# Six gather buffers in place of nine in a deformable-convolution and expert kernel

## The chip, the cores and the metric

The kernel runs on one core of a Trainium2 chip. The metric is the device time of one execution in microseconds (us). A core has a matrix engine (TensorE, PE in the profile), a vector engine (VectorE, DVE), an activation engine (ScalarE, ACT), GpSimd (POOL), and SyncE (SP), which issues most plain transfers. Each works through its own queue of instructions in order and waits on semaphores for the others. GpSimd here does hardly anything but issue gathers, that is, transfers whose source rows come from a list of indices.

## What is computed

The input `x` has 4 images of 256 channels and 64x64 pixels. It is normalised over channels, then goes through three deformable 3x3 convolutions (each samples 9 positions per pixel, displaced by offsets that a small ordinary convolution computes, and interpolates between four neighbours). The result is added to `x`. Each pixel then becomes a token of 256 values that goes through the two best of eight experts (256 to 512 to 256 with a GELU), and that is added too.

```
def _deform_layer(x, w_off, b_off, w, b, dilation=1):
    om = lax.conv_general_dilated(x, w_off, ...) + b_off[None, :, None, None]
    off = om[:, :2 * K].reshape(B, K, 2, H, W)
    mask = jax.nn.sigmoid(om[:, 2 * K:])
    ...
    sampled = _bilinear(x, ys, xs) * mask[:, None]
    out = jnp.einsum('bikhw,oik->bohw', sampled, wk) + b[None, :, None, None]
...
x = x + _L0_conv_ref(_ln_c(x), ...)
t = t + _L0_ffn_ref(_ln_t(t), ...)   # top 2 of 8 experts, weighted by softmax
```

## The kernel before

**Tiling.** A pixel block is 512 pixels (8 rows of an image, `BLK`), handled as 4 groups of 128 pixels on the 128 partitions. Per block, 9 taps times 4 groups make 36 samples; 3 layers x 4 images x 8 blocks x 36 = 3456 samples in all.

**One sample** (`samples`, from line 489). The features of a layer lie in a table in device memory, in which one row of 4 KB holds the four neighbours of a position, each of 256 float32 values. GpSimd gathers 128 such rows into a tile `g` of 4 KB per partition (line 503). VectorE interpolates between neighbours along one axis, in place (line 509), then along the other into a smaller tile `s` (line 514), which is the last reading of `g`. ScalarE scales `s` by the mask (line 517). TensorE transposes `s` (line 532), ScalarE copies the transposed pair of samples to `sT` (line 535), and TensorE multiplies it with the tap's weights and accumulates (line 549).

```
g = self.gat.tile([P, 2, 2, C], F32, tag="g", ...)
self.gathered = nc.gpsimd.indirect_dma_start(out=g..., in_=self.table(...), in_offset=...idx[:, j : j + 1]...)
nc.vector.scalar_tensor_tensor(g[:, :, 0, :], g[:, :, 1, :], cf[:, j, 0:1], g[:, :, 0, :], ...)
s = self.smp.tile([P, C], F32, tag="s", ...)
self.last = nc.vector.scalar_tensor_tensor(s, g[:, 1, 0, :], cf[:, j, 1:2], g[:, 0, 0, :], ...)
nc.scalar.activation(s, s, AF.Copy, scale=cf[:, j, 2:3])
```

**Buffers around it.** The pool `gat` gives out `GB` tiles `g` in turn (line 147); a gather into a tile has to wait until line 514 has read what was in it. `s` has 8 tiles, and TensorE takes pairs of samples `LAG` = 2 pairs after they are put into VectorE's queue. Tiles and the orders of the queues are worked out when the kernel is built, from the program's order and from which buffers are free.

**Who else uses the pool.** In the first phase the normalisation puts its input and output blocks into the same tiles (`room`, line 188). At the end, the last group of tokens gathers its experts' outputs into them (`combine_fetch`, line 911).

**Work in between.** The kernel weaves other work between the samples: the offset convolution of the next layer's blocks (`off_block`), storing a layer's result into the tables (`store_table`), token normalisation and routing (`tokens`, `route`, `invert`), the experts (`expert`), and the weighted sum of their outputs (`combine`). Three lanes hand out pieces of it per tap, at a pace per group of tokens. VectorE's pieces are put behind the newest `self.last`, GpSimd's behind the newest `self.gathered`. On GpSimd, one step of an expert fetches a weight tile `w` (line 803) and two token tiles `zt` (line 815), and the sums fetch `gy` (line 918), all in the same queue as the gathers. On VectorE, line 895 adds a bias to an expert's output `y`, and lines 395 to 427 work out positions, indices and coefficients of a later block.

Of the kernel before, what the change touches and what calls it, by code (L numbers as in the profile page):

```python
# [34 lines left out]
FT_LOG = 8  # L35
FT = 1 << FT_LOG
FU = FT // P
GB = 9
LAG = 2
LEAST = 2.0**-30  # L40
WINN = CC * (RPB + 2) * W
# [76 lines left out]
class Weave:  # L118
# [3 lines left out]
    def __init__(self, ctx, tc, ins, out):  # L122
# [7 lines left out]
        def pool(name, bufs, **kw):  # L130
            return ctx.enter_context(tc.tile_pool(name=name, bufs=bufs, **kw))
# [14 lines left out]
        self.smp = pool("smp", 8)  # L146
        self.gat = pool("gat", GB)
        self.ps = pool("ps", 3, space=bass.MemoryType.PSUM)
# [999 lines left out]
```

## Time and profile before

| | us |
|---|---|
| median of 3 runs | 6531.28 (6528.49 to 6531.62) |
| the profiled execution, its own time | 7434.65 |
| span of its page | 7432.9 |
| scaling `s`, line 517, ACT, 3456 times | 1630.8 busy |
| interpolation into `s`, line 514, DVE, 3456 times | 1656.7 busy |
| weights product, line 549, PE, 6912 times | 3442.6 busy |
| transposes of `s`, line 532, PE, 6912 times | 1227.0 busy |

The profile is of one execution, which took 14% longer than the runs without one. Rows of groups give the source line, the engine, what is written and read, how many instructions, their busy time and mean duration, and then the idle time of the engine before them with what ended it. "issue" there means that the profile shows nothing that was waited for. A busy TensorE isn't one at its peak[...].

### The profile page before, as it was taken

How to read it: one execution, taken by the hardware profiler on the slowest of the kernel's cores; microseconds unless marked ns; L12 is line 12 of the kernel's file. 1: busy time of each engine (PE TensorE's matmuls, PEld its weight loads, DVE VectorE, ACT ScalarE, POOL GpSimd, SP SyncE). 2: the span in 40 equal slices, each digit the busy share in tenths (PEclk: the TensorE clock that was granted, in tenths of full speed). 3: DMA queues.
4: the chain of work that ended last, by engine and by line, in shares of the span. 5: the costliest groups of instructions: out<-in, count | busy, mean ns of one | idle time of the engine just before them, and what ended most of it. 6: DMA issues, size and time to landing. Idle time of an engine off the chain costs nothing. (4 is left out here: it accounts for less than half of the span.)

```text
span 7432.9 us, 88104 instructions
## 1 busy us (share of the span) xinstructions
PE 6352.4 (85%) x26500; PEld 3653.7 (49%) x26500; DVE 4932.4 (66%) x11467; ACT 3278.3 (44%) x7139; POOL 4441.2 (60%) x4245
## 2 busy tenths in 40 slices
PE   7888888888888898988877898898887889977887
PEld 3434443444445555555444454454554456644665
DVE  7767776888756666776855676666787554667521
ACT  3444444554444444554443444444453334444322
POOL 4555665666656665555666665665667664666543
PEclk8999999989999999999989999999998899988988
DMA  8889999999879888888888998888998876887644
GB/s 286 312 297 339 346 339 346 362 345 340 321 267 322 311 315 315 310 314 296 282 295 306 327 331 299 318 324 314 325 342 307 281 273 233 286 301 271 229 138 124
DMA packets 805210, 2228.40 MB, mean 300 GB/s; under 512 B 105016, under 2 KB 307768, under 8 KB 798976
## 3 DMA queue, kind: packets, MB, share of 16 engines
q0 software_dynamic: 551200, 1947.35, 73.0%
q1 hardware_dynamic: 253536, 275.41, 11.0%
q8 instruction: 214, 3.51, 0.2%
q14 instruction: 260, 2.13, 0.1%
HBM read 2165.40 MB, written 196.40 MB: 318 GB/s over the span
## 5 line engine op out<-in xcount | busy, mean ns | idle before, releaser
L503 POOL DMA_INDIRECT g<-tab,idx x3456 | 3650.6, 1056 | 2310.7 <-DVE s L514 975.8
L549 PE MATMUL acc<-sT,wk 128*128 128x512 f32 x6912 | 3442.6, 620 | 44.6 <-ACT r L580 17.0
L509 DVE SCALAR_TENSOR_TENSOR g<-g,cf 128x512 f32<-128x512 f32 x3456 | 2556.5, 743 | 274.2 <-DMA g<-tab,idx 249.9
L514 DVE SCALAR_TENSOR_TENSOR s<-g,cf 128x256 f32<-128x256 f32 x3456 | 1656.7, 482 | 1287.5 <-PE tp L532 561.4
L535 ACT COPY sT<-tp 128x512 f32<-128x512 f32 x1728 | 1010.7, 586 | 2052.0 <-PE tp L532 1137.3
L532 PE MATMUL tp<-ident,s 128*128 128x128 f32 x6912 | 1227.0, 287 | 635.7 <-ACT s L517 373.8
L517 ACT ACTIVATE s<-s,cf 128x256 f32<-128x256 f32 x3456 | 1630.8, 508 | 260.7 <-DVE s L514 157.0
L549 PEld LDWEIGHTS acc<-sT,wk 128*128 128x128 f32 x6912 | 1238.3, 200 | 916.2 <-issue 871.5
L532 PEld LDWEIGHTS tp<-ident,s 128*128 128x128 f32 x6912 | 880.9, 147 | 1607.0 <-issue 839.5
L859 PE MATMUL ph<-fzT,w 128*128 128x256 f32 x2608 | 683.7, 401 | 111.1 <-ACT hT L869 74.2
L877 PE MATMUL py<-w,hT 128*128 128x256 f32 x2608 | 658.8, 392 | 39.9 <-ACT hT L869 23.2
L859 PEld LDWEIGHTS ph<-fzT,w 128*128 128x128 f32 x2608 | 498.1, 200 | 256.2 <-ACT hT L869 92.7
L869 ACT ACTIVATE hT<-ph,w 128x256 f32<-128x256 f32 x652 | 279.2, 471 | 695.2 <-PE ph L859 388.3
L877 PEld LDWEIGHTS py<-w,hT 128*128 128x128 f32 x2608 | 486.6, 194 | 180.6 <-issue 69.4
L815 POOL DMA_INDIRECT zt<-z,tok x326 | 330.9, 1015 | 174.2 <-issue 90.3
L803 POOL DMA_INDIRECT w<-in_W,wrow x163 | 175.7, 1078 | 379.3 <-ACT sT L535 134.1
L357 PE MATMUL po<-win,wo 128*32 128x504 f32 (+1 forms) x2304 | 364.1, 613 | 11.2 <-issue 8.3
L918 POOL DMA_INDIRECT gy<-ys,slots x256 | 260.2, 1017 | 106.7 <-issue 79.7
L895 DVE TENSOR_TENSOR y<-py,w 128x512 f32<-128x512 f32 x163 | 111.8, 686 | 316.3 <-PE py L877 242.7
L366 ACT ACTIVATE om<-po,bo 128x512 f32<-128x512 f32 x96 | 66.0, 688 | 365.4 <-PE po L357 228.5
L357 PE MATMUL po<-win_pre,wo 128*32 128x504 f32 (+1 forms) x1152 | 191.2, 628 | 4.1 <-ACT om L366 3.3
L357 PEld LDWEIGHTS po<-win,wo 128*32 128x32 f32 x2304 | 74.4, 111 | 223.8 <-issue 190.5
(154 smaller groups left out, 3029.2 us busy)
## 6 DMA issues: line engine op xcount, KB each, us to landing
tab<-hv SPq DMA_DIRECT2D x512, 128.0 KB
g<-tab,idx POOLq DMA_INDIRECT x3456
ys<-y SPq DMA_DIRECT2D x163, 256.0 KB
tab<-h_pre SPq DMA_DIRECT2D x128, 256.0 KB
wk<-in_conv_w SPq DMA_DIRECT2D x117, 256.0 KB
xc_pre<-in_x SPq DMA_DIRECT2D x32, 512.0 KB
xr_tok<-in_x SPq DMA_DIRECT2D x32, 512.0 KB
t<-t_tok SPq DMA_DIRECT2D x32, 512.0 KB
```

The source lines that it names most:

```text
L357: nc.tensor.matmul(po[g * Q : (g + 1) * Q, :].rearrange("q (r w) -> q r w", w=W)[:, :, x0:x1], lhsT=self.wo[l][:, 3 * ky + kx, c, :], rhs= ...
L503: self.gathered = nc.gpsimd.indirect_dma_start(out=g.rearrange("p x s f -> p (x s f)"), out_offset=None, in_=self.table(*self.stages[i][:2 ...
L509: nc.vector.scalar_tensor_tensor(g[:, :, 0, :], g[:, :, 1, :], cf[:, j, 0:1], g[:, :, 0, :], ALU.mult, ALU.add,)
L514: self.last = nc.vector.scalar_tensor_tensor(s, g[:, 1, 0, :], cf[:, j, 1:2], g[:, 0, 0, :], ALU.mult, ALU.add)
L517: nc.scalar.activation(s, s, AF.Copy, scale=cf[:, j, 2:3])
L532: self.turned = nc.tensor.transpose(tp[:, c, u * P : (u + 1) * P], ss[u][:, c * P : (c + 1) * P], self.ident)
L535: nc.scalar.copy(self.sT[:, :, t0 * P : (t0 + 2) * P], tp)
L549: nc.tensor.matmul(self.acc[:, o, :], lhsT=self.wk[k][:, c, o * P : (o + 1) * P], rhs=sT[:, c, :], start=(k == 0 and c == 0), stop=(k == K ...
L815: self.nc.gpsimd.indirect_dma_start(out=zt, out_offset=None, in_=grp.zd, in_offset=bass.IndirectOffsetOnAxis(ap=grp.tok[:, j : j + 1], axi ...
L859: nc.tensor.matmul(ph[:, h, :], lhsT=w1[:, o : o + P], rhs=zT[:, c, :], start=(c == 0), stop=(c == CC - 1),)
L869: nc.scalar.activation(ht[:, h, :], ph[:, h, :], AF.Gelu, bias=w1[:, k : k + 1])
L877: nc.tensor.matmul(py[:, u, :], lhsT=hT[h // 2][:, h % 2, u * P : (u + 1) * P], rhs=w2[:, h * C : (h + 1) * C], start=(h == 0), stop=(h == ...
```

## The change

One constant is changed. The pool has six tiles `g` of 4 KB per partition where it had nine, so a gather waits for line 514 of the sample six back, not nine back. The first phase and the last group of tokens, which borrow the tiles, have six too. No instruction's operation or shape changes, and the 12 KB per partition that this leaves over are not used.

```
 FU = FT // P
-GB = 9
+GB = 6
 LAG = 2
```

## The prediction

> **What bounds the kernel now.** I read the page first (engine shares, slices, groups), then the list of waits, then the gather tile `g` by itself, then two stretches of the timeline. The page's first part, in busy us, share of the span and number of instructions:
>
> ```profile
> span 7432.9 us, 88104 instructions
> PE 6352.4 (85%) x26500; PEld 3653.7 (49%) x26500; DVE 4932.4 (66%) x11467; ACT 3278.3 (44%) x7139; POOL 4441.2 (60%) x4245
> DMA  8889999999879888888888998888998876887644
> ```
>
> TensorE carries the span, but not alone: PE has some 1080 us idle, and the DMA engines are busy eight or nine tenths nearly everywhere. The gather is where the change acts. Two rows of the groups (busy and mean ns, then idle time ahead and what ended most of it):
>
> ```profile
> L503 POOL DMA_INDIRECT g<-tab,idx x3456 | 3650.6, 1056 | 2310.7 <-DVE s L514 975.8
> L509 DVE SCALAR_TENSOR_TENSOR g<-g,cf 128x512 f32<-128x512 f32 x3456 | 2556.5, 743 | 274.2 <-DMA g<-tab,idx 249.9
> ```
>
> GpSimd waits 975.8 us for a buffer (L514 is the last reader of `g`); VectorE waits only 249.9 us for a gather. So today the buffers are usually full and gathers are early. The list of waits (us in total, times, longest) says how often:
>
> ```profile
> ACT sT L535 <- PE tp L532: 1137.3, 843, 7.3
> POOL g L503 <- DVE s L514: 975.8, 457, 15.4
> POOL g L503 <- issue: 801.9, 2420, 2.5
> ...
> DVE s L514 <- PE tp L532: 561.4, 349, 9.7
> ...
> PE tp L532 <- ACT s L517: 373.8, 174, 15.9
> ...
> DVE g L509 <- DMA g<-tab,idx: 249.9, 98, 10.3
> ```
>
> VectorE runs dry 98 times in 3456. VectorE also waits for PE (561.4 us) more than PE waits for samples on this row (373.8 us): the two take turns holding each other. The tile's own answer, with first and last start:
>
> ```profile
> L503 POOL DMA_INDIRECT g<-tab,idx x3456: 940/974/5220, 90.2 to 6990.8; - x192
> L509 DVE SCALAR_TENSOR_TENSOR g<-g,cf x3456: 644/745/816, 94.4 to 6997.8; 128x512 f32<-128x512 f32 x192
> ```
>
> The first gather is used 4.2 us after GpSimd starts it (nothing else in the rings), the last 7.0 us after. The mean demand is (6997.8-94.4)/3456 = 2.00 us per gather. How fast gathers can follow each other, and what starvation looks like, from the timeline of GpSimd and of VectorE (start, duration, idle before):
>
> ```profile
> 6876.12 0.96 POOL L918 DMA_INDIRECT gy<-ys,slots  x1 [0.30 <-issue]
> 6877.38 0.95 POOL L503 DMA_INDIRECT g<-tab,idx  x1 [0.30 <-issue]
> 6878.63 0.95 POOL L503 DMA_INDIRECT g<-tab,idx  x1 [0.30 <-issue]
> ```
>
> ```profile
> 6882.40 0.75 DVE L509 SCALAR_TENSOR_TENSOR g<-g,cf 128x512 f32<-128x512 f32 x1 [6.83 <-DMA g<-tab,idx]
> 6883.29 0.48 DVE L514 SCALAR_TENSOR_TENSOR s<-g,cf 128x256 f32<-128x256 f32 x1
> ```
>
> GpSimd's burst rate is one gather per 1.25 us. The gather started at 6877.38 is used at 6882.40: 5.02 us, with VectorE standing 6.83 us for it.
>
> **What the Trainium skill says.** "DMA: Bandwidth & Descriptors", section "Anatomy of one DMA — SWDGE (gpsimd) path", fits a GpSimd DMA with 2.0 us plus bytes/436e3. A gather is 128 rows of 4 KB, 524288 bytes, so the estimate is 2.0+1.2 = 3.2 us. The first gather of the trace agrees: 4.2 us less 0.95 us on GpSimd is 3.25 us. The same page, "Issuing engines are not separate DMA queues", says that DMAs of all issuing engines interleave on the same 16 DMA engines; the growth from 4.2 to 5.0 and 7.0 us in traffic fits that, although no row separates the cause. "Perfetto Trace Analysis", section "Optimization Strategy", says that a gap that keeps recurring on the engine that ought to be saturated can mean too few buffers. In this trace the recurring buffer gap is on GpSimd, which isn't the saturated engine.
>
> **The change part by part.** No instruction is added or removed; 3 tiles of 4 KB per partition go.
>
> *Steady flow: nothing.* A buffer is held from the gather's start to the end of L514, and GpSimd takes it 0.27 us later (an L514 from 3007.70 to 3008.17 releases a gather at 3008.44). L509's start to L514's end is 1.37 us in the two lines above. The loop is thus 4.2+1.37+0.27 = 5.8 us empty, 6.7 us at the 5.02 us gather, 8.6 us at the last one's 7.0 us. Six buffers pass one gather per 0.97, 1.11 or 1.44 us; nine pass one per 0.65 to 0.96 us. All are under the mean demand of 2.00 us. What six lose is stock: GpSimd leads by up to 3 gathers less, 3x1.28 = 3.8 us in a burst and 6 us at mean demand.
>
> *Bursts.* VectorE does a sample in 1.28 us when it is free (L509 at 3018.11, 3019.39, 3020.67). At the 7.0 us end the six-buffer loop of 1.44 us is 0.16 us slower. GpSimd issued 2420 gathers back to back ("issue" above), so the most that this can cost is 2420x0.16 = 387 us; at 5.02 us per gather it costs nothing.
>
> *Cover for GpSimd's other work.* A fetch puts three other DMAs between gathers (3016.13 to 3021.29 instead of 1.28 us later: 3.9 us), 163 times over the kernel. Nine buffers hide that; with six, a loop of 6.7 us plus 3.9 us is 10.6 us for six samples, 1.77 us each: hidden at mean demand, 2.9 us short in a burst. Where the fetch itself waits for its weight buffer, nothing is lost: GpSimd comes to it with fewer gathers out, but it leaves at the same moment.
>
> *The sum.* The two overlap, so I count them together over the trace's rows. For each gather I move its start to 0.27 us after the end of the L514 six gathers back, where it was earlier than that, keep its landing time as the DMA packets show it, and compare with when L509 took it. 671 of 3456 L509s would then be late, in 242 runs whose largest latenesses sum to 270 us: 144 us before 1950 us (no fetch there yet), 126 us after. Of the first part most are threes in which L509 ran ahead of L514 by several samples while `s` had no room (L509 four times in a row at 1796.2 to 1798.5); there VectorE was about to stand anyway, so I keep a third, 48 us. VectorE is late by 174 us. How much reaches PE? There are eight `s` buffers and PE works two pairs behind, so short delays are absorbed when PE is behind. I take the ratio of the two opposite waits, 373.8/(373.8+561.4) = 0.40: 70 us. The profiled execution took 7434.65 us, so 7505 us; the three runs' median of 6531.28 us is 0.878 of it, and scaled the cost is 62 us: **6593 us**, 0.9% slower.
>
> *Later fetches.* The weight and token fetches stand in GpSimd's queue behind a gather that now starts later, by 4.8 us on average where it is moved. PE waits today 15.9+10.0 us for weights, so they mostly have room; their bound is 0 to 50 us, I take 0.
>
> *Start and tail.* The first phase borrows the same tiles for its input blocks; three blocks are loaded ahead and two more tiles are in use, which fits in six. In the tail, the last group's combine borrows up to eight in place of gathers; the seventh waits until the first is summed, some 24 fetches of 1.28 us later. Both at nothing; at most one 5 us landing each.
>
> **Rivals.**
> A. Absorbed: PE is 85% busy with a denser schedule unprofiled (6352 us of busy PE against a 6531 us run, if it were the same work), so VectorE's lateness is swallowed. Against it stand the 174 PE waits for samples. 6531 us, within 13 us.
> B. The loop becomes the bound in bursts, as at the 7.0 us gather: 387 us on VectorE, 0.7 of it through because PE then runs dry for long, 271 us profiled, 238 us scaled: 6770 us. For it: the DMA engines at nine tenths. Against: fewer gathers out also means shorter queues in the rings.
> C. Faster. The order of VectorE's queue is fixed when the kernel is built and depends on which buffers are then free. In 210 samples (counted in the rows) L509s stand ahead of an earlier sample's L514; with three buffers fewer, less of this 0.74 us work can stand ahead of the side work that PE and GpSimd wait for (the sum `y`, positions). If all of it moved back, 210x0.74 = 155 us of that work would come earlier; a quarter on PE's path is 39 us, 34 scaled: 6497 us. It decides if VectorE's wait for gathers grows by less than 39/0.40 = 98 us. Against it: the run-ahead happens where VectorE had nothing better to do.
>
> **How the numbers follow.** The forecast (slower by 0.2 to 2.5%) has 0.56, A 0.12, B 0.17, C 0.15. About 0.2% is what a measurement of this kernel can tell from no change. So faster 0.15, same 0.12, slower 0.73. The forecast's own range is 6545 to 6695 us; to leave no more than 2 in 10 out, it reaches to C's 6497 and halfway into B: 6495 to 6740 us.
>
> **What would show it.** VectorE's wait for gathers at L509 grows from 249.9 to 400 us or more and from 98 to 200 times or more; GpSimd's wait for L514 grows well over 975.8 us, to several thousand; PE's wait for `s` grows by some 70 us; busy times and counts stay. I am wrong if L509's wait stays under 350 us (A or C), or if L509's spacing in undisturbed bursts goes from 1.28 to 1.4 us (B), or if VectorE's order of L509 and L514 has changed so much that the rows can't be compared.

## The result and the profile after

With six buffers the kernel takes **6712.36 us** (median of 4 runs, 6705.84 to 6723.06) where it took 6531.03 us with nine: a ratio of 1.028 (95% interval 1.0264 to 1.0296), 181 us slower. The forecast was 6593 us. The sign was right and the time lies in the wider range, but the loss is three times the 62 us of the forecast.

One fact is needed to read the numbers below: the same kernel with nine buffers took about 6530 us in some groups of runs and 7404 to 7522 us in others, and the profile that the prediction was made from (7434.65 us) is of the long kind, so each experiment is compared only with the nine-buffer runs of its own group. What stands opposite the profile after (6723.06 us) is therefore a nine-buffer execution of 6529.06 us (`base_d`).

The page of the nine-buffer kernel in the short group, first its shares, then three of the groups:

```profile
span 6527.2 us, 88104 instructions
PE 6078.2 (93%) x26500; PEld 3548.0 (54%) x26500; DVE 4956.1 (76%) x11467; ACT 3327.0 (51%) x7139; POOL 4423.9 (68%) x4245
...
L503 POOL DMA_INDIRECT g<-tab,idx x3456 | 3623.7, 1049 | 1546.1 <-issue 602.0
...
L509 DVE SCALAR_TENSOR_TENSOR g<-g,cf 128x512 f32<-128x512 f32 x3456 | 2559.3, 743 | 465.5 <-DMA g<-tab,idx 459.7
...
L532 PE MATMUL tp<-ident,s 128*128 128x128 f32 x6912 | 1191.9, 280 | 194.9 <-ACT s L517 192.8
```

The same lines of the page after, with six:

```profile
span 6720.8 us, 88230 instructions
PE 6137.5 (91%) x26500; PEld 3551.9 (53%) x26500; DVE 5013.5 (75%) x11467; ACT 3363.6 (50%) x7139; POOL 4494.3 (67%) x4245
...
L503 POOL DMA_INDIRECT g<-tab,idx x3456 | 3688.7, 1067 | 1683.9 <-issue 536.4
...
L509 DVE SCALAR_TENSOR_TENSOR g<-g,cf 128x512 f32<-128x512 f32 x3456 | 2570.9, 745 | 865.4 <-DMA g<-tab,idx 852.0
...
L532 PE MATMUL tp<-ident,s 128*128 128x128 f32 x6912 | 1218.5, 281 | 305.2 <-ACT s L517 299.3
```

The counts of work are the same and the mean durations of the gather chain's work nearly so. What grows is idle time ahead of L509, by 400 us, and 392 us of that end on a gather. On TensorE, idle time (span less busy) goes from 6527.2-6078.2 = 449.0 to 6720.8-6137.5 = 583.3 us, 134 us more, of which the wait of L532 for `s` is 106.5 us. PE's busy time grows by 59 us for the same 26500 matmuls. The two, 193.6 us, are the difference of the spans.

The list of waits (us in total, times, longest), nine buffers:

```profile
...
ACT s L517 <- DVE s L514: 611.0, 663, 8.9
POOL g L503 <- issue: 602.0, 1926, 0.7
...
DVE g L509 <- DMA g<-tab,idx: 459.7, 407, 10.4
POOL g L503 <- DVE s L514: 361.2, 317, 12.8
```

and six:

```profile
...
ACT s L517 <- DVE s L514: 939.7, 1013, 8.8
DVE g L509 <- DMA g<-tab,idx: 852.0, 897, 10.3
...
POOL g L503 <- issue: 536.4, 1760, 0.3
POOL g L503 <- DVE s L514: 464.5, 406, 10.6
```

What grew is VectorE's wait for gathers: from 407 times to 897, +392 us. It passes to ScalarE (L517) almost undiminished, +329 us, and from there in part to TensorE. GpSimd's own wait for a buffer grows only from 361.2 to 464.5 us. The last column tells what sort of starvation it is: the longest wait has not grown, there are just many more short ones, 0.95 us each on average (852.0/897).

How fast samples are used, by the gather tile itself (first and last start), nine buffers and then six:

```profile
L509 DVE SCALAR_TENSOR_TENSOR g<-g,cf x3456: 642/744/821, 96.0 to 6109.5; 128x512 f32<-128x512 f32 x192
```

```profile
L509 DVE SCALAR_TENSOR_TENSOR g<-g,cf x3456: 645/746/821, 97.4 to 6303.2; 128x512 f32<-128x512 f32 x192
```

(6109.5-96.0)/3456 = 1.74 us per sample with nine, 1.80 us with six. In the profile of the prediction it was 2.00 us. The first sample comes 1.4 us later, and behind the last one the span goes on for 417.7 us with nine and 417.6 with six: the start and the tail cost next to nothing, as forecast. And by stage, for L509 alone (stretch, length, busy and number on VectorE, granted PE clock, share of the DMA engines, GB/s), nine buffers, then six:

```profile
100.00:1100.00 1000.00, 497.12 (x672) 0.99 1.01 391
1700.00:6300.00 4600.00, 1802.37 (x2429) 0.98 0.93 341
```

```profile
100.00:1100.00 1000.00, 477.13 (x642) 0.99 0.99 374
1700.00:6300.00 4600.00, 1844.70 (x2477) 0.98 0.93 341
```

In the first stretch, where no expert fetches its weights yet, nine buffers bring 672 samples in 1000 us, one per 1.49 us, with the DMA engines busy all the time (1.01). Six bring 642, one per 1.56 us. (The later stretch has more samples with six because more of them are then left to do.) Counted by sample over the rows, six are 94 us behind after 1080 of the 3456 samples, about when the first fetches come (1741.9 us with nine, 1709.8 us with six); 139 us after 2592; 194 us at the end. Half of the loss is thus made in a third of the samples, in a stage with hardly a fetch.

A stretch of that kind on VectorE with six buffers (start, duration, idle before):

```profile
1502.81 0.75 DVE L509 SCALAR_TENSOR_TENSOR g<-g,cf 128x512 f32<-128x512 f32 x1 [1.14 <-DMA g<-tab,idx]
1503.69 0.48 DVE L514 SCALAR_TENSOR_TENSOR s<-g,cf 128x256 f32<-128x256 f32 x1
1504.09 0.74 DVE L509 SCALAR_TENSOR_TENSOR g<-g,cf 128x512 f32<-128x512 f32 x1
1504.97 0.48 DVE L514 SCALAR_TENSOR_TENSOR s<-g,cf 128x256 f32<-128x256 f32 x1
1506.49 0.75 DVE L509 SCALAR_TENSOR_TENSOR g<-g,cf 128x512 f32<-128x512 f32 x1 [1.03 <-DMA g<-tab,idx]
```

and what TensorE does meanwhile:

```profile
1500.02 1.88 PE L549 MATMUL acc<-sT,wk 128*128 128x512 f32 x4
1501.73 0.97 PE L532 MATMUL tp<-ident,s 128*128 128x128 f32 x6
1504.77 0.64 PE L532 MATMUL tp<-ident,s 128*128 128x128 f32 x2 [2.06 <-ACT s L517]
```

In these lines VectorE waits about a microsecond for two gathers out of three, and PE stands 2.06 us for the sample that comes of it.

### The profile page after: what moved, and what is told of

Its sections match the earlier page's. It is cut to its first block, busy times and chain, and to the rows that moved or that the text cites. A ratio compares the mean times of both kernels' runs of the same rounds, so it can differ in the third digit from the quotient of the medians.

```text
span 6720.8 us, 88230 instructions
## 1 busy us (share of the span) xinstructions
PE 6137.5 (91%) x26500; PEld 3551.9 (53%) x26500; DVE 5013.5 (75%) x11467; ACT 3363.6 (50%) x7139; POOL 4494.3 (67%) x4245
## 5 line engine op out<-in xcount | busy, mean ns | idle before, releaser
L503 POOL DMA_INDIRECT g<-tab,idx x3456 | 3688.7, 1067 | 1683.9 <-issue 536.4
L549 PE MATMUL acc<-sT,wk 128*128 128x512 f32 x6912 | 3336.0, 603 | 13.7 <-ACT win L580 9.9
L509 DVE SCALAR_TENSOR_TENSOR g<-g,cf 128x512 f32<-128x512 f32 x3456 | 2570.9, 745 | 865.4 <-DMA g<-tab,idx 852.0
L517 ACT ACTIVATE s<-s,cf 128x256 f32<-128x256 f32 x3456 | 1691.2, 509 | 1019.8 <-DVE s L514 939.7
L514 DVE SCALAR_TENSOR_TENSOR s<-g,cf 128x256 f32<-128x256 f32 x3456 | 1657.7, 482 | 362.9 <-PE tp L532 49.5
L549 PEld LDWEIGHTS acc<-sT,wk 128*128 128x128 f32 x6912 | 1196.5, 194 | 839.9 <-issue 800.2
L535 ACT COPY sT<-tp 128x512 f32<-128x512 f32 x1728 | 1009.8, 585 | 1175.5 <-PE tp L532 1169.9
L532 PEld LDWEIGHTS tp<-ident,s 128*128 128x128 f32 x6912 | 867.8, 144 | 1246.5 <-ACT s L517 695.3
L532 PE MATMUL tp<-ident,s 128*128 128x128 f32 x6912 | 1218.5, 281 | 305.2 <-ACT s L517 299.3
L859 PE MATMUL ph<-fzT,w 128*128 128x256 f32 x2608 | 651.3, 386 | 29.2 <-DMA w<-in_W,wrow 17.0
L877 PE MATMUL py<-w,hT 128*128 128x256 f32 x2608 | 641.2, 385 | 20.6 <-ACT hT L869 14.8
L859 PEld LDWEIGHTS ph<-fzT,w 128*128 128x128 f32 x2608 | 478.3, 192 | 165.5 <-ACT hT L869 36.9
L357 PE MATMUL po<-win,wo 128*32 128x504 f32 (+1 forms) x2304 | 346.8, 595 | 0.8 <-ACT om L366 0.4
L933 DVE SCALAR_TENSOR_TENSOR ta<-gy,cw,ta 128x256 f32<-128x256 f32 x256 | 120.4, 478 | 97.7 <-DMA gy<-ys,slots 55.1
```

The source lines that it names most:

```text
L357: nc.tensor.matmul(po[g * Q : (g + 1) * Q, :].rearrange("q (r w) -> q r w", w=W)[:, :, x0:x1], lhsT=self.wo[l][:, 3 * ky + kx, c, :], rhs= ...
L503: self.gathered = nc.gpsimd.indirect_dma_start(out=g.rearrange("p x s f -> p (x s f)"), out_offset=None, in_=self.table(*self.stages[i][:2 ...
L532: self.turned = nc.tensor.transpose(tp[:, c, u * P : (u + 1) * P], ss[u][:, c * P : (c + 1) * P], self.ident)
L535: nc.scalar.copy(self.sT[:, :, t0 * P : (t0 + 2) * P], tp)
L549: nc.tensor.matmul(self.acc[:, o, :], lhsT=self.wk[k][:, c, o * P : (o + 1) * P], rhs=sT[:, c, :], start=(k == 0 and c == 0), stop=(k == K ...
L859: nc.tensor.matmul(ph[:, h, :], lhsT=w1[:, o : o + P], rhs=zT[:, c, :], start=(c == 0), stop=(c == CC - 1),)
```

## The experiments

Two theories stood at the start. The **loop**: a buffer's round (gather, landing, L509, L514, release) divided by the number of buffers comes too near to the pace at which samples are wanted. The **stock**: the round is short enough, but fewer samples lie ready when GpSimd is away at a fetch. Beside them stood the **order**: the queues, laid out when the kernel is built, differ with six buffers. Where "before" is named, it is the nine-buffer median of the same group.

### Group with 7522 us before

The nine-buffer kernel once more, for its profile.

> The kernel before, profiled once more, since its first profile (7434.65 us) took 14% longer than its other runs and the profile with six buffers did not (6723.06 us). If the first profile was unlike the others: span near 6530 us, PE clock near 0.97 instead of 0.932, and VectorE's wait for gathers at L509 below 150 us. If six buffers merely suffer less from profiling: span again near 7430 us.

7507.26 us, with a granted TensorE clock of 0.927 over the run. The group's other 43 nine-buffer runs have a median of 7521.97 us, so the long time is not a chance of one profiled execution.

Seven buffers:

```
-GB = 9
+GB = 7
```

> Seven buffers. Theory loop: a buffer is held 8.85 us on average with six (start of the gather to the end of L514), so six pass one gather in 1.48 us where VectorE could take one every 1.28 us; seven pass one in 1.26 us, so most of the 181 us is gone: 6531 to 6590 us. Theory stock (each buffer is one sample of slack between GpSimd and PE): a third of the loss comes back per buffer, 60 us, so about 6650 us. Theory order (the queues are put in another order when the kernel is built): no rule, somewhere between 6530 and 6715 us.

7511.13 us against 7521.97: 0.9986 (0.9971 to 1.0001), no loss.

Nine buffers, but the queues built as if a gather could not come before the L514 six samples back (the order alone, with no waiting for a buffer):

```
+            if len(self.ends) >= 6:
+                self.tc.add_manual_dep(
+                    self.gathered.ins, self.ends[-6].ins.name,
...
+                    reason="order",
+                )
...
+            self.ends.append(self.last)
```

> Nine buffers, but the queues are laid out nearly as with six (an ordering edge without a wait from each L514 to the gather six samples later): GpSimd's queue is identical to that with six, and VectorE's stands like it in 11115 of 11469 places. Theory loop and theory stock: 6531 us within 15. Theory order: about 6700 us.

7541.86 us: 1.0027 (1.0013 to 1.0041). The order is worth about a quarter of a per cent, and to the slower side. It is nearly that of six buffers: the rows have 179 samples whose L509 stands ahead of an earlier sample's L514, where six buffers have 176 and nine have 210.

Six buffers and 20 `s` tiles in the room that they leave:

```
-GB = 9
+GB = 6
...
-        self.smp = pool("smp", 8)
+        self.smp = pool("smp", 20)
```

> Six gather buffers, and the 12 KB that they leave over go to 12 further tiles s (20 in place of 8). Theory loop: s is not in the loop from gather to L514, so 6690 to 6720 us. Theory stock: 26 samples of slack in place of 17, so 6560 us or less. Theory order: between these.

7924.8 us: 1.0522 (1.0484 to 1.056), a loss of a size that neither theory explains.

With seven buffers free of cost here and these 5% for a deeper `s`, this group did not look like the run that had lost 2.8%. So the next group has six buffers beside nine.

### Group with 7404 us before

> The kernel before once more, beside six buffers on one chip. The first two profiles of it (7432.9 and 7505.4 us) had TensorE at half clock for 1008 and 1095 us, the profile with six buffers (6720.8 us) for 395 us. Theory chip: these two chips grant different clocks, and on a chip where the kernel takes near 6531 us its half-clock time is under 400 us; on a chip where it takes near 7520 us it is about 1000 us again.

> Six buffers, the change itself. Theory loop: on a chip where the kernel before takes 6531 us, 6712 us within 15. On a chip where it takes about 7520 us, TensorE asks for a sample only every 2.0 us, so VectorE waits less for gathers and the loss shrinks: 7540 to 7600 us. Theory stock: the loss is the same 181 us or more on both, since deeper TensorE pauses need more slack.

The nine-buffer profile took 7390.86 us. The changed kernel itself took 7260.65 us against 7403.56: 0.9803 (0.9783 to 0.9823). In this group six buffers are 2% **faster**, where both theories had expected a loss. The list of waits, nine buffers:

```profile
POOL g L503 <- DVE s L514: 959.3, 475, 15.4
...
ACT sT L535 <- remote: 525.4, 124, 17.5
DVE s L514 <- remote: 347.8, 127, 13.9
...
DVE g L509 <- DMA g<-tab,idx: 253.4, 106, 10.3
```

six:

```profile
POOL g L503 <- DVE s L514: 799.4, 436, 17.0
DVE g L509 <- DMA g<-tab,idx: 505.3, 427, 10.2
ACT sT L535 <- remote: 483.0, 124, 17.5
...
DVE s L514 <- remote: 217.2, 100, 8.5
```

VectorE's wait for gathers doubles here too (+252 us), so the changed kernel starves in the same place. But the run holds another loss, the "remote" rows: ScalarE's copy L535, and VectorE's L514, wait up to 17 us for something that none of the core's engines is shown to release. Such rows of this size exist in the profile of the prediction (608.4 us on L535) and in neither profile of the short group. A place of that kind, on ScalarE and then on TensorE, nine buffers:

```profile
376.13 1.04 PE L442 MATMUL tp_pre<-ident,xc_pre 128*128 128x128 f32 x8
...
377.22 1.88 PE L549 MATMUL acc<-sT,wk 128*128 128x512 f32 x4
...
382.59 0.58 ACT L447 COPY h_pre<-tp_pre 128x512 f32<-128x512 f32 x1 [6.39 <-remote]
...
384.90 1.11 PE L532 MATMUL tp<-ident,s 128*128 128x128 f32 x4 [5.80 <-ACT s L517]
...
385.81 3.24 PE L549 MATMUL acc<-sT,wk 128*128 128x512 f32 x4
```

The transposes that L447 copies (L442) had ended by TensorE's rows at 377.2 us; ScalarE got them at 382.59. What stands behind L447 waited too, TensorE for 5.80 us, and its four products then took 3.24 us where the four before the stop had taken 1.88. The last part is what the Trainium skill describes in "TensorE: Matmul & The Clock Gate", section "Part 1: The HAM clock gate (the "warmup" mystery)": after an idle window of about 3.4 us TensorE's clock is at half until it has been busy for about as long. The trace agrees: TensorE is 5.80 us idle and then slower by 1.7 times, with a mean granted clock of 0.56 from 385 to 389 us. Of the 1728 copies L535, those that came over 3 us after TensorE's rows had ended were 160 with nine buffers in this group, 130 with six, and 4 in `base_d` (88, 66 and 0 of them with ScalarE idle all that time); time at half clock was 1016, 931 and 332 us. With six there are fewer such stops, and that fits the gain; why they occur at all, and why fewer gathers in flight should mean fewer of them, the runs don't settle.

The prediction was thus made from a profile in which TensorE was held up by a thing that the timed runs don't have.

### Group with 6530 us before

Nine buffers for the profile (above), seven, four, and six with gathers of half the size.

> Nine buffers, profiled on a third chip. Two chips so far took 7522 and 7404 us for it, and there TensorE's results come over 3 us later than its records end 160 times; the forecast was measured where it takes 6531 us. If this chip is like the latter, both theories expect VectorE's wait for gathers at L509 under 150 us and TensorE's half-clock time under 400 us; otherwise about 253 us and 1015 us as in the profile before.

> Seven buffers. Theory loop (a buffer's round takes 8.85 us, VectorE's own pace is 1.28 us): where nine take 6531 us, 6540 to 6590 us; where nine take about 7400 us, as nine within 0.3%. Theory stock (a third of the loss per buffer): 6652 us where nine take 6531 us; and where six gain 2.0% (7404 us), a gain of about 1.3%.

> Four buffers. Theory loop: a round of 7 to 8 us over four gives one gather in 1.75 to 2.0 us in every stretch, 3456 of them 6050 to 6900 us and 420 us of tail: 6700 to 7500 us on any chip, so well slower where nine take 6531 us and at most 3% slower where they take 7400 us. Theory stops (a faster stream makes TensorE stop more often on the slow chips, and fewer buffers prevent it): faster than nine on a slow chip, with fewer than 100 late results.

Seven: 6585.4 us against 6529.6, 1.008 (1.0063 to 1.0096), in the range of the loop and not of the stock. Four: 7871.75 us, 1.2051 (1.2028 to 1.2073), above the loop's 7500 us; whether four would be faster than nine in a long group stays untried. Together with nine and six the curve is 7872, 6712, 6585, 6530 us for 4, 6, 7 and 9 buffers: steep below seven and flat above. Four buffers' waits show the end of that road:

```profile
DVE g L509 <- DMA g<-tab,idx: 1928.0, 1899, 10.2
POOL g L503 <- DVE s L514: 1697.2, 1208, 10.1
```

Only there do both ends of the loop wait for each other for about as long, each for over a fifth of the time. From the rows I counted how long a buffer is held, from the start of its gather to the end of L514. A part of that is no need of the loop: the gather has landed (the last of its 16 semaphore updates has come) and the full buffer waits until VectorE takes it. The fourth column leaves that part out, adds the 0.27 us from a release to the next gather, and divides by the number of buffers, so it is the pace at which the loop could run by itself:

| buffers | mean round, us | of it full and waiting, us | loop by itself, us per gather | L509 spacing, mean us | time, us |
|---|---|---|---|---|---|
| 4 | 7.56 | 0.19 | 1.91 | 2.13 | 7872 |
| 6 | 8.85 | 0.66 | 1.41 | 1.80 | 6712 |
| 7 | 9.74 | 1.21 | 1.26 | 1.76 | 6585 |
| 9 | 11.53 | 2.58 | 1.02 | 1.74 | 6530 |

The round grows with the number of buffers, in part because a full buffer waits longer to be read. The fourth column against the pace of VectorE and of the stage tells the cost. VectorE can take one sample per 1.28 us when it is free: nine buffers pass gathers well faster than that, seven just so, six don't. The first stretch (100 to 1100 us) takes one sample per 1.49 us on average with nine buffers; there the loop by itself needs 1.13 us with nine, 1.31 with seven and 1.42 with six, which leaves little for bursts. The whole round divided by the number of buffers would mislead: for nine in the long group it is 14.91/9 = 1.66 us, slower than any of this, and yet seven cost nothing in such a group.

Half-size gathers leave out the lower of each pair of neighbours: a row of 2 KB lands in half of `g`, and L509 reads it in the place of both.

```
-                out=g.rearrange("p x s f -> p (x s f)"),
+                out=g[:, 0].rearrange("p s f -> p (s f)"),
...
-                g[:, :, 0, :], g[:, :, 1, :], cf[:, j, 0:1], g[:, :, 0, :],
-                ALU.mult, ALU.add,
+                g[:, 1], g[:, 0], cf[:, j, 0:1], g[:, 0], ALU.mult, ALU.add,
...
-                s, g[:, 1, 0, :], cf[:, j, 1:2], g[:, 0, 0, :], ALU.mult, ALU.add
+                s, g[:, 1, 0, :], cf[:, j, 1:2], g[:, 1, 1, :], ALU.mult, ALU.add
```

> Six buffers, and each gather brings 2 KB per row in place of 4 KB (the lower pair of neighbours is left out and the upper pair takes its place, so the output differs); instructions and their shapes stay. Theory loop: packets are half as long, so a round shrinks by 1 us or more and the DMA engines are a third less busy: where nine take 6531 us, within 1% of that again. Where nine take about 7400 us, theory stops: no better than six, 7230 us or more.

7718.0 us, 1.1824 (1.1796 to 1.1851): slower by 18% with half the bytes, the largest miss of the study. The time from gather to L509 fell to 3.94 us (median) where it is 7.2 us with six full-size buffers, but up to six L509 now stood in a row before the first L514, so that the round rose to 10.23 us. That this order of VectorE's queue is the cause is shown by the next group, where the same kernel with L509 kept in its place takes 6571.96 us. The list of waits:

```profile
ACT s L516 <- DVE s L513: 2723.4, 1307, 9.8
DVE g L509 <- DMA g<-tab,idx: 2229.5, 1933, 10.3
```

This run says nothing about the bytes; it says that running ahead with L509 holds buffers.

### Group with 6534 us before

The order alone again, now in the short group; then half-size gathers with L509 kept behind the sample before it, at six and at nine buffers; then the deeper `s` again.

> Nine buffers with the queues laid out nearly as with six. Where nine take about 6530 us: theory loop and theory stock 6530 us within 20; theory order 6680 us or more. Where nine take 7400 us or more: within 0.5% of nine, as measured once (1.0027).

6542.19 us: 1.0012 (1.0003 to 1.0021). The order explains next to nothing of the 2.8%.

```
+            with self.after(self.last):
+                nc.vector.scalar_tensor_tensor(
+                    g[:, 1], g[:, 0], cf[:, j, 0:1], g[:, 0], ALU.mult, ALU.add,
+                )
```

> Six buffers, gathers of 2 KB per row (the lower neighbours are left out, the upper ones take their place), and L509 of a sample is kept behind L514 of the sample before, since without that the halved gather let the queues be laid out with up to six L509s in a row (that run took 7718 us). Theory loop: from a gather's start to L509 it is 4 us in place of 7.2 us, a round is 5.5 us, six pass one gather in 0.9 us, below VectorE's 1.28 us: within 0.4% of the same kernel with nine buffers. Theory stock: 2 to 3% slower than that.

> The same with nine buffers: the yardstick for the run before. No theory sets its own time, since the build lays the other work out anew; 6350 to 6650 us where nine full gathers take 6530 us.

Six: 6571.96 us, 1.0052 (1.0035 to 1.0069). Nine: 6506.34 us, 0.9964 (0.9949 to 0.9978). With half the bytes the three buffers are worth 65.6 us, 1.0%, in place of 181 us. The loop theory had at most 0.4% here, the stock theory 2 to 3%: neither is right alone. The rows of waits, six and nine:

```profile
DVE g L510 <- DMA g<-tab,idx: 247.3, 185, 9.8
```

```profile
DVE g L510 <- DMA g<-tab,idx: 107.4, 69, 9.7
```

In the half-size pair's profiles the difference is 32 us after 1080 samples, 72 us after 1944 and 90 us at the last, so most of it comes once there are fetches, and not before them as at full size. I read it so: about 65 us of the 181 is what a fetch uncovers, and the rest goes with the length of the landing. The half-size pair alone doesn't prove it, since that kernel also moves fewer bytes for everybody else, but the rows of the profiles bear it out. From each L509 that waited for its gather, go back along GpSimd's queue to the first gather that started within 0.6 us of its buffer's release (the loop held it) or the first that stands behind another transfer of GpSimd (a fetch held it). VectorE's wait then divides so:

| kernel | behind a buffer, us | behind a fetch, us | all, us |
|---|---|---|---|
| nine (`base_d`) | 6 | 421 | 459.7 |
| seven (`gb7_d`) | 83 | 494 | 612 |
| six (`after`) | 225 | 572 | 852.0 |
| nine, half-size (`gb9_half_strict_e`) | 0 | 97 | 107.4 |
| six, half-size (`gb6_half_strict_e`) | 3 | 216 | 247.3 |

Of the 392 us that six full-size buffers add, some 220 are the loop and 150 the lost cover; at half size 119 of the 140 us that six add are lost cover and 3 the loop.

> Six gather buffers and 20 tiles s in place of 8 (on a chip where nine take 7522 us this took 7925 us). Where nine take about 6530 us: theory loop 6690 to 6740 us, as six alone; theory stock 6560 us or less; if the deep s queue by itself harms, as on the slow chip by 5%, 6850 us or more.

6679.06 us: 1.0219 (1.0202 to 1.0236), just below the loop's range and far above the stock's. Where it had cost 5% in the long group, the deeper `s` gives back some 35 of the 181 us here. VectorE's wait for gathers is as long as before:

```profile
DVE g L509 <- DMA g<-tab,idx: 880.1, 912, 10.5
```

More tiles `s` don't help much when it is the gathers that don't come: a longer store behind the bottleneck stays empty. Why it costs 5% in the long group stays open.

### Groups with 7512 and 6532 us before

If the round matters and not the number of tiles as such, then freeing `g` earlier must recover part of the loss. Here L509 writes into a small pool of its own of 2 KB tiles, so that `g` is free after L509 and doesn't wait for L514:

```
-GB = 9
+GB, HB = 6, 4
...
+            h = self.hp.tile([P, 2, C], F32, tag="h", ...)
...
-                g[:, :, 0, :], g[:, :, 1, :], cf[:, j, 0:1], g[:, :, 0, :],
+                h, g[:, :, 1, :], cf[:, j, 0:1], g[:, :, 0, :], ALU.mult, ALU.add,
...
-                s, g[:, 1, 0, :], cf[:, j, 1:2], g[:, 0, 0, :], ALU.mult, ALU.add
+                s, h[:, 1, :], cf[:, j, 1:2], h[:, 0, :], ALU.mult, ALU.add
```

> Six gather buffers; L509 writes into a tile h of its own (2 KB, four of them), so that a buffer comes free 0.53 us earlier, after L509. Where nine take about 6530 us: theory loop, the round goes from 8.85 to about 8.3 us, 1.39 us per gather, the same as the 9.74 us of seven over seven: 6580 to 6630 us. If the number of buffers alone counts: 6712 us within 15.

> The kernel of gb6_h4_f once more. Where nine take about 6530 us: theory loop 6580 to 6630 us; if the number of buffers alone counts, 6712 us within 15. Where nine take about 7500 us: again about 1% faster than nine.

In the long group 7443.98 us against 7511.92, 0.9892 (0.9864 to 0.9921). In the short group **6612.65 us** against 6532.36, 1.0134 (1.0117 to 1.0151): 80 us slower than nine, in the loop's range, where six plain buffers are 181 us slower. The waits there:

```profile
DVE h L510 <- DMA g<-tab,idx: 704.8, 709, 10.6
```

The loop by itself now needs 1.31 us per gather, which falls between six (1.41, +181 us) and seven (1.26, +55 us); a straight line between those two gives about +97 us, and +80 were measured. Divided as above, 127 us of VectorE's wait come behind a buffer (225 with six plain ones) and 516 behind a fetch. It is the same six tiles, the same gathers and the same fetches. The tiles `h` also change the order of VectorE's queue a little, but the order alone was worth 0.12%.

Two other uses of the same room were tried in the long group: eight `g` with two `h` (8 and 2 in the diff above), and ten `g` with two `sT` in place of three.

```
-GB = 9
+GB = 10
...
-        self.smT = pool("smT", 3)
+        self.smT = pool("smT", 2)
```

> Eight gather buffers and two tiles h, in the memory of nine buffers. Where nine take about 6530 us: theory loop, eight count as about eight and a half, 6530 to 6560 us; two tiles h let L509 run ahead of L514 by two samples at most. Faster than nine only if below 6515 us.

> Ten buffers, paid for by two in place of three tiles sT. Where nine take about 6530 us: theory loop, the curve goes on to flatten (181, 55, 0 us over nine for six, seven, nine): 5 to 20 us gained by the tenth, if sT doesn't cost it; if TensorE needs the third sT, slower than 6545 us.

7574.72 us, 1.0078 (1.0053 to 1.0103), and 7551.34 us, 1.0045 (1.0027 to 1.0062), both slower by less than 1%. Their forecasts were for a short group, where they were not tried. In the short groups no full-size version was faster than nine buffers; in the long ones none gained more than the six plain buffers did (0.9803).

## Why the prediction was right in direction and wrong in size

**The mechanism holds.** Nothing was added to the work; VectorE runs dry at L509 more often, ScalarE and TensorE follow. L509's wait went over both marks set for it (852.0 us and 897 times, for 400 and 200). Start and tail cost next to nothing. Seven and four buffers and the earlier release of `g` put the larger part of the cost in the round of the buffers, and the rest in the lost cover for fetches, the two things that the prediction counted together. That the sign came out right was in part luck: in runs like the profile that the prediction was made from, six buffers are faster (0.9803).

**"Steady flow: nothing" failed.** It set the loop of 1.44 us at most against a demand of 2.00 us, and saw 0.56 us of room. The loop was about right (1.41 us measured); the demand was not. Where the kernel is timed it is 1.74 us, and 1.49 us in the first stretch, where the loop of six needs 1.42 us. There is hardly any room, and 94 of the 194 us between the spans arise there.

**"The sum" is where the number went wrong**, in three terms that multiply. Taken one after the other:

| term | predicted | measured | sum after it, us |
|---|---|---|---|
| as predicted: 174 us x 0.40 x 0.878 | | | 61 |
| the first part kept to a third | 174 us in all (270 counted) | +252 us in the long group | 270 x 0.40 x 0.878 = 95 |
| lateness scaled down by 0.878 from the long profile | 270 x 0.878 = 237 us | +392 us in the short group | 392 x 0.40 = 157 |
| share that reaches the end | 0.40 | 193.6/392 = 0.49 | 194 |

The uncut count of 270 us agrees with the +252 us measured in the long group. Cutting the early part from 144 to 48 us, since VectorE "was about to stand anyway", was the wrong choice: over the first 1080 samples the wait grew there from 12 to 118 us. The largest term is the second. The profile was 14% longer than the runs, and the prediction scaled the loss down by that 0.878, as if the long execution had been the same work drawn out. It was the opposite: the long execution had stops of TensorE, during which gathers caught up (a buffer of the nine is held for 14.9 us on average in the long group and for 11.5 us in `base_d`), and with them taken out the loss grows. In the profile itself the signs were the 608.4 us in the "remote" row of L535 and the clock of 0.932, beside a TensorE only 85% busy.

**The share** was the ratio of two opposite waits of the long profile, 0.40; it measured 0.49. That the two are near is luck rather than a rule: in the long group itself +252 us of that wait went with a span 110 us shorter. Of the 193.6 us that reach the end, 134 are PE's idle time and 59 its longer busy time, 27 of them on the transposes L532, which follow the waits. Half-clock time grew by 63 us.

**GpSimd's wait for L514** was expected to grow to several thousand us. It grew by 103 us, and all of GpSimd's idle time ahead of gathers by 138 us (1546.1 to 1683.9). The gathers do start later: 2386 of the 3456 start while the other five tiles are all in use, where with nine 1326 start while the other eight are. But a gather that starts later is not a GpSimd that stands idle for as long, as each late start also moves the next; with four buffers the wait is 1697.2 us.

**The rivals.** A (absorbed) and C (faster by the order) are refuted in the short group, C also by the order alone at 1.0012. B, the loop as the bound in bursts, forecast 6770 us and came nearer than the forecast. Its sign was seen in part: spacings of L509 up to 1.31 us fell from 1713 to 1295, those of 1.31 to 1.6 us rose from 504 to 649. Its 387 us on VectorE are close to the 392 us measured, but by luck, as only some 220 of these are the loop. As stated it isn't right either, since most of VectorE's wait is in single gaps of about a microsecond, not in a burst slowed throughout. And C's result, faster, is what the long group shows, by another mechanism than C's.

**Later fetches**, taken at nothing, cost TensorE nothing that the profiles show: its waits at L859 for weights (PE and PEld) are 33.3 us with nine buffers and 30.3 us with six.

## What to carry to other kernels

Count how long a buffer is needed, from the start of its transfer to the landing and from the first reading to the release, without the time that it stands full; divide by the number of buffers and compare it with the pace of the densest stage, not with the mean over the kernel. Here, against 1.49 us in that stage, nine buffers needed 1.13 us, seven 1.31 us and cost 0.8%, six 1.42 us and cost 2.8%. Then add what the other work in the issuing queue uncovers, which was over a third of the added wait here. Before that, see whether the profiled execution is like the timed ones: when it is 14% longer, a sum made on it can't be scaled, and even its sign may not carry. And a shorter hold is worth nearly as much as another buffer: releasing `g` one instruction earlier gave back 100 of 181 us, a seventh buffer 126.

## What the runs showed that was not expected

- One kernel, one input, one core: about 6530 us in the runs of the result and in three further groups, 7404 to 7522 us in three others, each steady within its group (6520.54 to 6538.07 us in one, 7487.52 to 7559.6 us in another). With nine buffers in the long ones, 160 or more of TensorE's results reach ScalarE over 3 us late, and TensorE is at half clock for about 1000 us. The long traces also hold about half as many recorded semaphore updates for the same program (61473 in `base_c`, 109967 in `base_d`), which may be why their releasers are so often "remote". The long groups ran on chips numbered 2, 4 and 5, the short ones on 4, 14 and 13; if the number 4 means one chip both times, the chip isn't the cause. The cause is open.
- In the long groups, fewer gathers in flight helped: six buffers at 0.9803, and early release with six at 0.9892.
- A gather of 512 KB that has 4.2 us from start to use when nothing else is in the rings has landed after 6.5 us (median) with six buffers and after 7.2 us with nine, with DMA engines 93 to 101% busy. The Trainium skill's "DMA: Bandwidth & Descriptors", section "Anatomy of one DMA — SWDGE (gpsimd) path", gives an estimate of 3.2 us for its size, to which 0.95 us on GpSimd come; together that is about the 4.2 us of the first gather, and far less than the later ones took. On average 0.66 us more pass in a full buffer with six, 2.58 us with nine.
